# Layer 0's attention on one Trainium2 core: score and value products of 512 columns instead of 256

## The chip, the cores and the metric

The kernel runs as one program on one core of a Trainium2 chip. The metric is the device time of one execution in microseconds, lower is better; the time before is the median of three runs. In the text PE is TensorE (matrix products; PEld are its weight loads), DVE is VectorE, ACT is ScalarE, POOL is GpSimd and SP is the engine that issues most DMAs. PSUM is the memory that PE writes its results to.

## The reference, cut to what matters

Two transformer layers over 8 sequences of 256 tokens with 128 channels, all in fp32. Each layer adds an attention and a mixture of experts, both of the same normalised input. The change touches only the attention of layer 0, with 16 heads of 8 channels:

```python
q, k, v = (proj(Wq, bq), proj(Wk, bk), proj(Wv, bv))     # (B, H=16, S=256, D=8)
scores = jnp.einsum('bhsd,bhtd->bhst', q, k) / jnp.sqrt(jnp.float32(D))
attn = jax.nn.softmax(scores, axis=-1)
out = jnp.einsum('bhst,bhtd->bhsd', attn, v)
x = x + out.reshape(B, S, E) @ Wo + bo + layer0_experts(xn)
```

Layer 0's experts (two of eight per token, and a shared one) and the whole of layer 1 (attention with 8 heads of 128 channels, one of eight experts per token) stay as they are.

## The kernel before

**Heads as rows.** The projections give queries and keys turned, channels on the 128 partitions and tokens along the row. The weight columns are reordered so that partition 32j + 8g + d holds channel d of head 4g + j: four bands of 32 partitions (j), each with four groups (g) of 8 channels. A score product of one head runs on one band of PE, 32 rows high, so four products on different bands can run at the same time. As a band holds four heads, `l0_project` writes four masked copies of the queries and four of the keys, one per group, with the other groups' rows put to zero by a column of ones and zeros (`own`). A block of 512 tokens (two sequences) therefore has 2 x 4 copies of 128x512. For block 0 DVE makes the queries' and ACT the keys' copies, for block 1 ACT makes all eight, for blocks 2 and 3 ACT copies the PSUM result once for each of the two (L566) and POOL makes the eight copies (L569).

**Two passes.** For the softmax's maximum, `max_scores` (L894) computes the scores with queries on the partitions and `max_rows` (L909) reduces them to minus the maximum, which goes into `mx`. `l0_augment` turns `mx` by two PE transposes (L918), and four DVE instructions (L921), one per group, add the maximum of a group to the queries in rows that belong to the next group; the copies of the keys hold ones in these rows (`turn`), so the second score product (`exp_scores`, L940) comes out with the maximum already taken off. ACT takes exponentials of 128x1024 at a time (L952). `l0_pv` (L967) multiplies them by the values. A value product has only 32 columns of weights, so four products run side by side on the columns of PE; they take 32 columns from `va_flat`, which are a head's 8 values, a one for the softmax's sum, and the next heads' columns, which are not used. `l0_normalise` turns the result by a DVE transpose in blocks of 32 and divides by the sum.

**The order.** For each sequence b there are eight units i (group g and half, a half being two bands). A unit issues four maximum products of sequence b + 1 and four score products of sequence b on the other two bands, in two rounds of two and two (`issue`), each product 256 columns wide; then the maximum reduction on DVE and the exponential on ACT. The maximum products write one PSUM tile of 128x1024 and the score products another. The pool has two such tiles, both taken by a unit and taken over by the next, so that a unit's maximum products wait for the reduction of the unit before, and its score products for the exponential before. After the second unit of a group `late` is set, and the value products of that group run in the unit that follows (`l0_drain`).

**What lies between.** `plan` is a table, written by hand, of places (two to each unit) at which other work is put into the same in-order engine queues: routing at the first places, then the 39 tiles of layer 0's experts (`l0_tile`, about five tiles to four units: a down product L709, four up products L692, one transpose L685, with the ACT instructions L718, L676 and L687), then the shared expert (L745, L760), the gathers of expert results, the norm of layer 1 and its first projections (L807). At i = 2 and i = 4 of an even sequence the loop projects the next block's queries and keys (L561). Those small products share three PSUM banks in turn (`bank`), so that a new one waits for the reader of the third before it. `keep_warm` (L1009) puts in products whose result nobody reads.

**The beginning.** Before the loop the eight maximum units of sequence 0 are issued in pairs (`first_scores`), without score products. The last sequence has score products without maximum products. All instructions of an engine run in the order of the program.

Of the kernel before, what the change touches and what calls it, by code (L numbers as in the profile page):

```python
# [10 lines left out]
F32 = mybir.dt.float32  # L11
# [4 lines left out]
ALU = mybir.AluOpType  # L16
# [46 lines left out]
def two_layer_kernel(  # L63
# [85 lines left out]

    hb = ctile([P, 2], "hb")  # L150
# [6 lines left out]
    qkb = ctile([P, 2, NG], "qkb")  # L157
# [5 lines left out]
    for g in range(NG):  # L163
        at = D0 * ((g + 1) % NG)
        seq(nc.vector.tensor_reduce(
            turn[:, g : g + 1],
            ident.rearrange("p (j r) -> p j r", r=ROW)[:, :, at],
            AX.X,
            ALU.add,
        ))  # L170
# [368 lines left out]
    def l0_values(blk):  # L539
        for t2 in range(blk * TPB, (blk + 1) * TPB, 2):  # L540
            ps = bank(f"vg_{t2}")
            pv = ps[:, : 2 * (E + NE + 1)].rearrange("p (t c) -> p t c", t=2)
            for t in range(2):
                seq(nc.tensor.matmul(
                    pv[:, t, :], lhsT=xT[:, ts(t2 + t, P)], rhs=wvg0_s, start=True, stop=True
                ))
            for t in range(2):
                seq(nc.scalar.copy(
                    va[:, t2 + t, :, :D0], pv[:, t, :E].rearrange("p (h d) -> p h d", d=D0)
                ))  # L550
            seq(nc.vector.tensor_copy(lg0[:, ds(t2, 2), :], pv[:, :, E:]))

    def l0_project(blk, n):


        if n == 0:
            both = work.tile([P, 2, NG, BLK], F32, tag="qk", name=f"qk0_{blk}")
            qk[blk] = (both[:, 0], both[:, 1])
        dst = qk[blk][n]
        ps = bank(f"qk0_{blk}_{n}")  # L560
        seq(nc.tensor.matmul(  # L561
            ps, lhsT=(wq0_p, wk0_p)[n], rhs=xT[:, ts(blk, BLK)], start=True, stop=True
        ))
        if blk > 1:
            both = work.tile([P, BLK], F32, tag="xn", name=f"qk0_all_{blk}_{n}")
            seq(nc.scalar.copy(both, ps))  # L566
        for g in range(NG):
            if blk > 1 or (blk == 0 and n == 0):
                seq((nc.gpsimd if blk else nc.vector).tensor_scalar(  # L569
                    dst[:, g, :],  # L570
                    both if blk else ps,
                    own[:, g : g + 1],
                    qkb[:, n, g : g + 1],
                    ALU.mult,
                    ALU.add,
                ))
            else:
                seq(nc.scalar.activation(
                    dst[:, g, :],
                    ps,  # L580
                    AF.Identity,
                    bias=qkb[:, n, g : g + 1],
                    scale=own[:, g : g + 1],
                ))
# [299 lines left out]

    def max_scores(b, i, ps):

        g, half = divmod(i, 2)
        qT, kT = qk[b // 2]
        o = (b % 2) * S
        pv = ps.rearrange("p (j t k) -> p j t k", j=2, t=2)  # L890

        def mm(t, jj):
            r = ROW * (2 * half + jj)
            seq(nc.tensor.matmul(  # L894
                pv[:, jj, t, :],
                lhsT=qT[r : r + ROW, g, ds(o + t * P, P)],
                rhs=kT[r : r + ROW, g, ds(o, S)],
                start=True,
                stop=True,
            ))  # L900

        return [(mm, t, jj) for t in range(2) for jj in range(2)]

    def max_rows(b, i, ps):

        g, half = divmod(i, 2)
        pv = ps.rearrange("p (j t k) -> p j t k", j=2, t=2)
        m = mx[b % 2].rearrange("p t (j r) -> p j t r", r=ROW)
        seq(nc.vector.tensor_reduce(  # L909
            m[:, ds(2 * half, 2), :, D0 * ((g + 1) % NG)], pv, AX.X, ALU.max, negate=True  # L910
        ))

    def l0_augment(b):

        qT, _ = qk[b // 2]
        ps = bank(f"mT_{b}")
        for t in range(2):
            seq(nc.tensor.transpose(ps[:, ts(t, P)], mx[b % 2][:, t, :], ident))  # L918
        qa = work.tile([P, NG, S], F32, tag="h", name=f"qa_{b}")
        for g in range(NG):  # L920
            seq(nc.vector.scalar_tensor_tensor(  # L921
                qa[:, g, :],
                ps[:, :S],
                turn[:, g : g + 1],
                qT[:, g, ds((b % 2) * S, S)],
                ALU.mult,
                ALU.add,
            ))
        return qa

    def exp_scores(b, i, qa, ps):

        g, half = divmod(i, 2)
        _, kT = qk[b // 2]
        o = (b % 2) * S
        pv = ps.rearrange("p (j c q) -> p j c q", j=2, c=2)

        def mm(c, jj):
            r = ROW * (2 * half + jj)
            seq(nc.tensor.matmul(  # L940
                pv[:, jj, c, :],
                lhsT=kT[r : r + ROW, g, ds(o + c * P, P)],
                rhs=qa[r : r + ROW, g, :],
                start=True,
                stop=True,
            ))

        return [(mm, c, jj) for c in range(2) for jj in range(2)]

    def exponentials(b, i, ps):  # L950
        eT = work.tile([P, 2, 2, S], F32, tag="e", name=f"eT_{b}_{i}", bufs=4)
        seq(nc.scalar.activation(eT.rearrange("p j c q -> p (j c q)"), ps, AF.Exp, scale=SC0))  # L952
        return eT

    def issue(*lists):

        for n in range(0, 4, 2):
            for calls in lists:
                for f, *args in calls[n : n + 2]:
                    f(*args)  # L960

    def l0_pv(b, g, eTs, po):

        for c in range(2):
            for j in range(4):
                o = ((2 * b + c) * H0 + 4 * g + j) * VW
                seq(nc.tensor.matmul(  # L967
                    po[ds(ROW * j, ROW), ts(g % 2, S)],
                    lhsT=va_flat[:, ds(o, ROW)],
                    rhs=eTs[j // 2][:, j % 2, c, :],  # L970
                    start=(c == 0),
                    stop=(c == 1),
                ))
# [3 lines left out]
    def l0_normalise(b, gp, po, at):  # L977

        nm = f"{b}_{gp}"
        ot = work.tile([P, 2, NQ, ROW], F32, tag="c", name=f"ot0_{nm}")  # L980
        seq(nc.vector.transpose(ot.rearrange("p g n r -> p (g n r)"), po))
        rec = small.tile([P, 2, NQ], F32, tag="rec0", name=f"rec0_{nm}")
        seq(nc.vector.reciprocal(rec, ot[:, :, :, D0]))
        seq(nc.vector.tensor_tensor(
            at[:, :, ds(2 * gp, 2), :].rearrange("p n g d -> p g n d"),
            ot[:, :, :, :D0],
# [29 lines left out]
    def first_maxima(i, pair):  # L1016
# [11 lines left out]
    seq(nc.vector.tensor_scalar(qkb[:, 0, :], own, hb[:, 0:1], None, ALU.mult))  # L1028
    seq(nc.vector.scalar_tensor_tensor(
        qkb[:, 1, :], own, hb[:, 1:2], turn, ALU.mult, ALU.add  # L1030
    ))
# [4 lines left out]
    l0_project(0, 0)  # L1036
    l0_project(0, 1)
# [20 lines left out]
    pair = first_scores(6)  # L1058
    next(routing0)
# [16 lines left out]
    def l0_drain(b, g, eTs, po, at):  # L1076
        l0_pv(b, g, eTs, po)
        if g % 2 == 1:
            l0_normalise(b, g // 2, po, at)
# [4 lines left out]
    late = None  # L1084
    keep_warm(3)
    qa = l0_augment(0)
    for b in range(B):
        at = work.tile([P, NQ, NG, D0], F32, tag="at0", name=f"at0_{b}")
        for g in range(NG):
            if g % 2 == 0:  # L1090
                po = held(f"pv0_{b}_{g}")
            eTs = []
            for half in range(2):

                i, i1 = 2 * g + half, 2 * g + 1 - half
                place = 2 * (b * NI + i)
                lists = []
                if b + 1 < B:
                    ps1 = big_tile(f"s1_{b + 1}_{i1}")
                    lists.append(max_scores(b + 1, i1, ps1))  # L1100
                ps2 = big_tile(f"s2_{b}_{i}")
                issue(*lists, exp_scores(b, i, qa, ps2))
                if b + 1 < B:
                    max_rows(b + 1, i1, ps1)
                eTs.append(exponentials(b, i, ps2))
                between(place)
                if b % 2 == 0 and b + 2 < B and i in (2, 4):
                    l0_project(b // 2 + 1, i // 2 - 1)
                if i == NI - 1 and b + 1 < B:
                    qa = l0_augment(b + 1)  # L1110
                if half == 0 and late is not None:
                    l0_drain(*late)
                    if g == 1 and done is not None:
                        l0_finish(*done)
                        done = None
                if i == 1 and done is not None:
                    done = (done[0], l0_turn_back(*done))
                between(place + 1)
            late = (b, g, eTs, po, at)
        done = (b, at)  # L1120
# [473 lines left out]
```

## Time and profile before

| What | Value |
|---|---|
| runs, us | 594.53, 591.26, 590.09; median 591.26 |
| profiled execution, us | 584.82 |
| its span, us | 583.0 |
| mean granted PE clock | 0.938 |
| PE, PEld busy, us | 497.3, 354.1 |
| DVE, ACT, POOL busy, us | 359.4, 246.6, 205.6 |
| PE instructions in the profile | 3996 products and 3996 weight loads |

The span is the time from the first to the last instruction of the profiled execution; 1.8 us of its time lie outside. Every fp32 product of the program appears as two records, each with a weight load and the full number of columns. A row of the groups gives line, engine, operation, tiles and shapes, the count, the busy time in us, the mean duration of one in ns, and then the idle time of the engine just before these instructions with what ended it. Products overlap, so that the count times the mean is more than the busy time where several run side by side.

### The profile page before, as it was taken

What the parts mean: (1) busy time and instruction counts of PE and PEld (TensorE: products, weight loads), DVE (VectorE), ACT (ScalarE), POOL (GpSimd) and SP (SyncE); (2) the same over time, 40 slices, a digit from 0 to 9 for tenths busy, and PEclk for the clock granted to TensorE, in tenths of its full rate; (3) what the DMA queues carried; (4) which work ended last, traced back from release to release, by engine and by line L of the source; (5) the groups of instructions that cost most, each with busy time, mean ns of one, the idle gap of its engine ahead of it and who ended that gap; (6) DMA issues with size and microseconds to landing.
All of it is one profiled execution on the core that took longest, in us unless ns stands there. A gap on an engine that the chain in (4) does not pass through costs nothing.

```text
span 583.0 us, 11267 instructions
## 1 busy us (share of the span) xinstructions
PE 497.3 (85%) x3996; PEld 354.1 (61%) x3996; DVE 359.4 (62%) x733; ACT 246.6 (42%) x681; POOL 205.6 (35%) x254
## 2 busy tenths in 40 slices
PE   4887688889998899967899968877969989989777
PEld 1633345656766577543554736666667878978666
DVE  5487954646756467637797467787633544527662
ACT  4616123434443254313443551523255584665161
POOL 6230023266432440274372032212576041124740
PEclk9999786989999799989999997996989999999977
DMA  3600411324443231011021130171048465512111
GB/s 108 189 1 19 133 33 44 110 72 121 126 128 105 74 77 38 28 46 29 17 69 45 37 92 19 37 200 41 25 108 234 145 149 180 158 55 64 33 32 56
DMA packets 61925, 47.78 MB, mean 82 GB/s; under 512 B 6389, under 2 KB 56781, under 8 KB 61869
## 3 DMA queue, kind: packets, MB, share of 16 engines
q1 hardware_dynamic: 57453, 38.59, 23.3%
q0 software_dynamic: 3840, 8.26, 5.9%
q8 instruction: 32, 0.52, 0.4%
q10 hardware_dynamic: 576, 0.20, 0.1%
q14 instruction: 24, 0.20, 0.1%
HBM read 38.78 MB, written 8.26 MB: 81 GB/s over the span
## 4 chain that ended last, share of the span: by engine, by line
PE 56%; DVE 20%; issue 9%; ACT 6%; POOL 4%; DMA 1%; SPq 0%; another core or an unknown queue 0%; POOLq 0%; ACTq 0%; DVEq 0%
PE s L894 7%; PE u L692 6%; PE pv L967 5%; PE s L1281 4%; PE d L709 4%; DVE mx L909 4%; PE u L1210 3%; PE o L1345 3%; PE d L1228 3%; PE qk L807 3%; PE s L940 3%; PE wo L1364 3%; ACT p L1301 2%; PE ds L760 2%; PE sh L745 2%
## 5 line engine op out<-in xcount | busy, mean ns | idle before, releaser
L952 ACT ACTIVATE eT<-s 128x1024 f32<-128x1024 f32 x64 | 65.5, 1024 | 138.9 <-PE s L940 95.7
L909 DVE TENSOR_REDUCE mx<-s 128x4 f32<-128x1024 f32 x64 | 77.7, 1220 | 32.0 <-PE s L940 14.3
L513 POOL DMA_INDIRECT xs<-xd,idx x62 | 63.0, 1016 | 67.0 <-issue 57.8
L894 PE MATMUL s<-qk 32*128 32x256 f32 x512 | 74.4, 422 | 13.6 <-DVE mx L909 8.8
L1313 POOL TENSOR_TENSOR p<-p,rec 128x1024 f32<-128x1024 f32 x21 | 39.8, 1896 | 112.3 <-DVE rec L1311 112.2
L1301 ACT ACTIVATE p<-s,m 128x256 f32<-128x256 f32 (+1 forms) x128 | 52.5, 443 | 62.5 <-DVE m L1295 51.0
L940 PE MATMUL s<-qa,qk 32*128 32x256 f32 x512 | 75.6, 414 | 2.5 <-DVE qa L921 2.3
L894 PEld LDWEIGHTS s<-qk 32*128 32x128 f32 x512 | 43.2, 195 | 41.7 <-DVE mx L909 17.9
L513 POOL DMA_INDIRECT yt<-yg,idx x48 | 48.9, 1020 | 47.1 <-issue 37.2
L1281 PE MATMUL s<-kT,qT 128*128 128x128 f32 (+1 forms) x256 | 49.8, 348 | 9.1 <-ACT p L1301 4.3
L940 PEld LDWEIGHTS s<-qa,qk 32*128 32x128 f32 x512 | 45.9, 192 | 10.6 <-DVE qa L921 5.0
L1345 PE MATMUL o<-pT,vrep 32*128 32x256 f32 x576 | 48.9, 407 | 3.9 <-DVE pT L1328 2.2
L1281 PEld LDWEIGHTS s<-kT,qT 128*128 128x128 f32 x256 | 40.0, 200 | 18.2 <-issue 6.9
L1345 PEld LDWEIGHTS o<-pT,vrep 32*128 32x128 f32 x576 | 40.5, 197 | 11.6 <-DVE pT L1328 2.4
L692 PE MATMUL u<-xg,gu_s 128*88 128x128 f32 x312 | 42.6, 278 | 1.6 <-issue 1.6
L967 PE MATMUL pv<-eT,va 128*32 128x256 f32 x512 | 39.3, 412 | 1.5 <-issue 1.4
L692 PEld LDWEIGHTS u<-xg,gu_s 128*88 128x88 f32 x312 | 37.1, 160 | 3.8 <-issue 3.8
L1219 ACT ACTIVATE h<-u,own_b 128x128 f32<-128x128 f32 x92 | 25.9, 375 | 27.7 <-PE u L1210 25.2
L1291 DVE TENSOR_TENSOR s<-s,mask 128x512 f32<-128x512 f32 (+1 forms) x24 | 20.9, 869 | 25.2 <-PE s L1281 21.5
L1364 PE MATMUL wo<-wo_s,oT 128*128 128x128 f32 x256 | 34.0, 297 | 2.1 <-DVE qT L814 1.8
L1364 PEld LDWEIGHTS wo<-wo_s,oT 128*128 128x128 f32 x256 | 33.0, 212 | 3.9 <-issue 3.3
L1328 DVE STREAM_TRANSPOSE pT<-p 128x1024 f32<-128x1024 f32 x24 | 29.5, 1232 | 7.1 <-POOL p L1313 7.1
(222 smaller groups left out, 843.2 us busy)
## 6 DMA issues: line engine op xcount, KB each, us to landing
w_up<-in_w_dram SPq DMA_DIRECT2D x30, 256.0 KB
gu_s<-in_gu_dram SPq DMA_DIRECT2D x39, 176.0 KB
vrep<-vd SPq DMA_DIRECT2D x32, 128.0 KB
w_down<-in_w_dram SPq DMA_DIRECT2D x16, 256.0 KB
yg<-ys SPq DMA_DIRECT2D x14, 256.0 KB
dn_s<-in_dn_dram SPq DMA_DIRECT2D x39, 88.0 KB
bias<-in_b_dram SPq DMA_DIRECT2D x23, 64.0 KB
acc<-in_x_dram SPq DMA_DIRECT2D x4, 256.0 KB
```

The source lines that it names most:

```text
L513: seq(nc.gpsimd.indirect_dma_start(out=dst, out_offset=None, in_=table, in_offset=bass.IndirectOffsetOnAxis(ap=idx[:, k : k + 1], axis=0), ...
L692: seq(nc.tensor.matmul(ps[:IC, ts(c, P)], lhsT=gu0_s[:, i % RING0, c, :], rhs=xg0.get(i), start=True, stop=True,))
L894: seq(nc.tensor.matmul(pv[:, jj, t, :], lhsT=qT[r : r + ROW, g, ds(o + t * P, P)], rhs=kT[r : r + ROW, g, ds(o, S)], start=True, stop=True,))
L909: seq(nc.vector.tensor_reduce(m[:, ds(2 * half, 2), :, D0 * ((g + 1) % NG)], pv, AX.X, ALU.max, negate=True))
L940: seq(nc.tensor.matmul(pv[:, jj, c, :], lhsT=kT[r : r + ROW, g, ds(o + c * P, P)], rhs=qa[r : r + ROW, g, :], start=True, stop=True,))
L952: seq(nc.scalar.activation(eT.rearrange("p j c q -> p (j c q)"), ps, AF.Exp, scale=SC0))
L967: seq(nc.tensor.matmul(po[ds(ROW * j, ROW), ts(g % 2, S)], lhsT=va_flat[:, ds(o, ROW)], rhs=eTs[j // 2][:, j % 2, c, :], start=(c == 0), s ...
L1281: seq(nc.tensor.matmul(u.sc[:, h, :], lhsT=qT[:, u.h0 + h, ds(o + u.t * P, P)], rhs=kT[:, ds(o, u.nk)], start=True, stop=True,))
L1301: seq(nc.scalar.activation(u.p[:, h, :], u.sc[:, h, :], AF.Exp, bias=u.m[:, h : h + 1], accum_out=u.sums[:, h : h + 1],))
L1313: seq(engine.tensor_tensor(u.p, u.p, rec[:, : u.nh].unsqueeze(2).to_broadcast([P, u.nh, u.nk]), ALU.mult))
L1345: seq(nc.tensor.matmul(po[n][:, ts(t, H1 * ROW)], lhsT=vrep[r : r + ROW, b % 2, j, :], rhs=pT[r : r + ROW, :, j, :], start=(j == 0), stop= ...
L1364: seq(nc.tensor.matmul(ps[:, ts(t, P)], lhsT=oT[:, h, ts(t, P)], rhs=wo1_s[:, h, :], start=(h == 0), stop=(h == H1 - 1),))
```

## The change

The unit of work becomes two groups of heads side by side. The query side is left unmasked for the maximum (one tile of 128x512 for a block, `l0_queries`), and the keys are masked in two ways (`l0_keys`): four copies by group (`kg`), of which two stand side by side as the moving operand of a maximum product, and two copies by pair of groups (`k2`), which are the weights of the score product. The queries of the score product are masked by group for each sequence by four ACT instructions of 128x256 (`l0_own_queries`), one in each of the units 1 to 4 of the sequence before, and the maximum is added in place by the same four DVE instructions as before. Maxima now go to the rows of the other pair of groups. A unit (`unit`: pair n, half of the tokens t or c, half of the bands) has two maximum and two score products of 512 columns each. Value products take 512 columns as well, two groups of one band side by side, with the values reordered so that both heads' columns lie next to each other; the two results of a band then lie in different rows, and `l0_normalise` reads the second with an offset of 9. The masked keys are made by ACT for all blocks, after block 0 one copy to a unit, and POOL takes no more part in it. The key projection moves from unit 4 to unit 3.

```diff
-    def l0_project(blk, n):
-        if n == 0:
-            both = work.tile([P, 2, NG, BLK], F32, tag="qk", name=f"qk0_{blk}")
-            qk[blk] = (both[:, 0], both[:, 1])
...
-        if blk > 1:
-            both = work.tile([P, BLK], F32, tag="xn", name=f"qk0_all_{blk}_{n}")
             seq(nc.scalar.copy(both, ps))
-        for g in range(NG):
-            if blk > 1 or (blk == 0 and n == 0):
-                seq((nc.gpsimd if blk else nc.vector).tensor_scalar(
...
+    def l0_queries(blk):
+        both = work.tile([P, 1 + NG + NG // 2, BLK], F32, tag="qk", name=f"qk0_{blk}")
+        qk[blk] = (both[:, 0], both[:, 1 : 1 + NG], both[:, 1 + NG :])
+        ps = bank(f"q0_{blk}")
+        seq(nc.tensor.matmul(ps, lhsT=wq0_p, rhs=xT[:, ts(blk, BLK)], start=True, stop=True))
+        seq(nc.scalar.activation(qk[blk][0], ps, AF.Identity, bias=hb[:, 0:1]))
+
+    def l0_keys(blk):
+        ps = bank(f"k0_{blk}")
+        seq(nc.tensor.matmul(ps, lhsT=wk0_p, rhs=xT[:, ts(blk, BLK)], start=True, stop=True))
+        if blk:
+            both = work.tile([P, BLK], F32, tag="xn", name=f"k0_all_{blk}")
+            seq(nc.scalar.copy(both, ps))
+            ps = both
+            yield
+        _, kg, k2 = qk[blk]
+        copies = [(kg[:, g, :], own[:, g : g + 1], kb[:, g : g + 1]) for g in range(NG)]
+        copies += [(k2[:, n, :], own2[:, n : n + 1], kb2[:, n : n + 1]) for n in range(NG // 2)]
+        for n, (dst, scale, bias) in enumerate(copies):
+            if blk == 0 and n < 2:
+                seq(nc.vector.tensor_scalar(dst, ps, scale, bias, ALU.mult, ALU.add))
             else:
+                seq(nc.scalar.activation(dst, ps, AF.Identity, bias=bias, scale=scale))
+            if blk:
+                yield
+
+    def l0_own_queries(b, g):
+        seq(nc.scalar.activation(
+            qas[b % 2][:, g, :],
+            qk[b // 2][0][:, ds((b % 2) * S, S)],
+            AF.Copy,
+            scale=own[:, g : g + 1],
+        ))
...
+    def unit(i):
+        return i // 4, i // 2 % 2, i % 2
...
-        def mm(t, jj):
+        def mm(jj):
             r = ROW * (2 * half + jj)
             seq(nc.tensor.matmul(
-                pv[:, jj, t, :],
-                lhsT=qT[r : r + ROW, g, ds(o + t * P, P)],
-                rhs=kT[r : r + ROW, g, ds(o, S)],
+                ps[:, ts(jj, 2 * S)],
+                lhsT=qT[r : r + ROW, ds(o + t * P, P)],
+                rhs=kg[r : r + ROW, ds(2 * n, 2), ds(o, S)],
...
-                lhsT=kT[r : r + ROW, g, ds(o + c * P, P)],
-                rhs=qa[r : r + ROW, g, :],
+                lhsT=k2[r : r + ROW, n, ds(o + c * P, P)],
+                rhs=qa[r : r + ROW, ds(2 * n, 2), :],
...
-    def l0_pv(b, g, eTs, po):
-        for c in range(2):
-            for j in range(4):
-                o = ((2 * b + c) * H0 + 4 * g + j) * VW
-                seq(nc.tensor.matmul(
-                    po[ds(ROW * j, ROW), ts(g % 2, S)],
-                    lhsT=va_flat[:, ds(o, ROW)],
-                    rhs=eTs[j // 2][:, j % 2, c, :],
+    def l0_pv(b, n, c, eTs, po):
+        for j in range(4):
+            o = ((2 * b + c) * H0 + NG * j + 2 * n) * VW
+            seq(nc.tensor.matmul(
+                po[ds(ROW * j, ROW), :],
+                lhsT=va_flat[:, ds(o, ROW)],
+                rhs=eTs[j // 2][:, j % 2].rearrange("p g q -> p (g q)"),
...
+            if b + 1 < B and NG > i - 1 >= 0:
+                l0_own_queries(b + 1, i - 1)
+            if b % 2 == 0 and b + 2 < B and i == 2:
+                l0_queries(b // 2 + 1)
+            if b % 2 == 0 and b + 2 < B and i == 3:
+                keys = l0_keys(b // 2 + 1)
+            if keys is not None:
+                next(keys, None)
             if i == NI - 1 and b + 1 < B:
                 qa = l0_augment(b + 1)
             if half == 0 and late is not None:
                 l0_drain(*late)
```

The four own queries of sequence 0 are made before the loop, after the last pair of maximum units is issued. The value products still run once in two units, and number half as many.

## The prediction

> **What bounds the kernel now.** I read the profile from the whole to the stage: first busy time by stretches, then the costliest groups, then the order of time inside one unit, then what PE waited for. Layer 0's attention runs from about 36 to 333 us. This view has one line for each stretch: length, then busy us and instructions of PE, PEld, DVE, ACT and POOL, PE clock, DMA share, GB/s.
>
> ```profile
> 36.00:88.00 52.00, 39.53 (x340) 19.58 (x339) 40.76 (x102) 16.76 (x19) 8.59 (x10) 0.89 0.18 52
> 88.00:216.00 128.00, 115.98 (x1098) 82.46 (x1099) 75.49 (x140) 52.95 (x129) 54.99 (x66) 0.92 0.36 96
> 216.00:333.00 117.00, 105.41 (x836) 62.27 (x836) 81.34 (x174) 45.27 (x83) 44.24 (x58) 0.99 0.15 39
> ```
>
> From 88 to 333 us PE is busy 221.4 of 245 us, so PE sets the pace there. From 36 to 88 us (routing) DVE and PE take turns. ACT works less than half of each stretch. What the change must shorten is therefore PE's own time, or the 23.6 us that PE still waits after 88 us.
>
> ```profile
> L894 PE MATMUL s<-qk 32*128 32x256 f32 x512 | 74.4, 422 | 13.6 <-DVE mx L909 8.8
> L940 PE MATMUL s<-qa,qk 32*128 32x256 f32 x512 | 75.6, 414 | 2.5 <-DVE qa L921 2.3
> L967 PE MATMUL pv<-eT,va 128*32 128x256 f32 x512 | 39.3, 412 | 1.5 <-issue 1.4
> L894 PEld LDWEIGHTS s<-qk 32*128 32x128 f32 x512 | 43.2, 195 | 41.7 <-DVE mx L909 17.9
> ```
>
> These are the products concerned. L894 and L940 lie over each other (512 x 422 ns would be 216 us), so their sum isn't PE's cost. The timeline of one unit (start, us, what) says how they run:
>
> ```profile
> 139.57 0.48 PE L894 MATMUL s<-qk 32*128 32x256 f32 x2
> 139.58 0.48 PE L940 MATMUL s<-qa,qk 32*128 32x256 f32 x2
> 139.89 0.38 PE L894 MATMUL s<-qk 32*128 32x256 f32 x2
> 139.90 0.38 PE L940 MATMUL s<-qa,qk 32*128 32x256 f32 x2
> 140.10 0.38 PE L894 MATMUL s<-qk 32*128 32x256 f32 x2
> ...
> 140.32 0.38 PE L894 MATMUL s<-qk 32*128 32x256 f32 x2
> ...
> 140.65 0.71 PE L709 MATMUL d<-dn_s,h 88*128 88x128 f32 x4
> ```
>
> Sixteen records go in four rounds of four, all four bands at once. A round takes 0.215 us (139.89 to 140.10 to 140.32), the first 0.32, and the next work starts 0.33 after the last: 1.08 us in all, of which 4 x 0.215 = 0.86 are columns and 0.22 belong to start and end. Weight loads of the next round lie under the running one.
>
> **The products (the heart of the change).** A unit will have 8 records of 512 columns, two rounds of four. What does a record of 512 columns take? The chain of waits has six in a row:
>
> ```profile
> 488.80 2.58 PE qk L807 x6
> ```
>
> 2.58 / 6 = 0.43 us, twice 0.215. So the unit is 2 x 0.43 + 0.22 = 1.08 us, as before. Value products: 16 records in four rounds now, 8 in two rounds then, 0.86 us either way, in 32 calls. The weight loads halve (768 of 3996 go), but all but the first of each unit are covered by a running round, and the first stays. If each round has a few ns of its own, two rounds less in 64 units and 32 calls are 192 x 3 ns, about 0.5 us; I take -0.5.
>
> Here a rule of the Trainium skill says otherwise: "TensorE: Matmul & The Clock Gate", section "Back-to-back issue gap", gives a sustained spacing of 81 ns per product at 128 columns and 131 ns at 512, so wide products would be far cheaper per column. Estimate by that page: about 98 ns at 256 columns, two of these against 131, a third less; of 0.86 us x (64 + 32) = 83 us that would be -27 us. The row above (0.43 against 0.215) decides: cost per column is the same here.
>
> **The wait for the queries of the next sequence.** At each turn of sequence PE waits for L921, four DVE instructions 0.39 us apart:
>
> ```profile
> 147.21 0.70 PE L894 MATMUL s<-qk 32*128 32x256 f32 x4
> 147.94 1.65 DVE L921 SCALAR_TENSOR_TENSOR qa<-mT,turn,qk 128x256 f32<-128x256 f32 x4
> 148.47 0.19 PEld L940 LDWEIGHTS s<-qa,qk 32*128 32x128 f32 x2 [0.95 <-DVE qa L921]
> ```
>
> The first score product reads one group and starts 0.53 us after the first of the four. Now its moving operand is two groups, so it starts after the second: +0.39 us. What PE has left then is the same: before, 1.06 us (148.47 to 149.53); after, both maximum products have run alone and the score products take two rounds, 1.08. Behind this wait on PE's queue stand the expert tile, the value products and the next unit. In six of the eight turns (from 36, 73, 110, 147, 183 and 221 us) the products began 0.53 us after the first L921, so were held by it; in the last two PE was late for other reasons. 6 x 0.39 = +2.4 us.
>
> **ACT.**
>
> ```profile
> L578 ACT ACTIVATE qk<-qk,qkb,own 128x512 f32<-128x512 f32 x12 | 8.4, 776 | 2.3 <-PE qk L561 2.3
> L566 ACT COPY qk_all<-qk 128x512 f32<-128x512 f32 x4 | 2.3, 586 | 3.5 <-PE qk L561 3.5
> L569 POOL TENSOR_SCALAR qk<-qk_all,own,qkb 128x512 f32<-128x512 f32 x16 | 12.2, 777 | 18.0 <-ACT qk_all L566 18.0
> ```
>
> Own queries: 32 of 128x256. No such row is there; L676 (256 wide, no scale by column) takes 0.381 us and L1301's 256 wide form 0.509. I take 0.49, nearer to the latter, as both read a column: +15.7 us. Blocks 2 and 3: one query copy (0.68, between L566 and L578), one L566 (0.586) and six copies of 0.776 are 5.9 us in place of 2 x 0.586 = 1.2, so +9.4 for two. Block 1: 5.9 in place of 8 x 0.776 = 6.2, -0.3. Block 0: five in place of four, +0.7, but the query copy falls into ACT's gap at 13.0 to 13.8 us, while DVE loses two of its four. ACT gets +25.5 us, POOL loses 12.2 us.
>
> How much comes out? ACT lies on PE's way where PE waits for a PSUM bank or for an exponential. From 88 to 216 us:
>
> ```profile
> PE s L894 <- issue: 4.6, 2, 3.9
> PE qk L561 <- ACT ys L718: 4.1, 2, 2.4
> ...
> PE mT L918 <- ACT ys L718: 1.3, 2, 0.6
> PE d L709 <- ACT ys L718: 0.7, 1, 0.7
> ```
>
> PE waited 6.1 us for 52.95 us of ACT's work, 11.5%. The same share of 25.5 is +2.9 us. The own queries stand after the expert tile's ACT work and ahead of the next exponential; where ACT is idle there, nothing comes out (end 0), and where none is hidden, all 25.5. I stay near the lower end since ACT is busy only 41% of that stretch. Section "Rules for kernel authors" of the skill's "ScalarE: Activation LUTs" speaks against this placing: multiply and add belong on VectorE, up to about three times faster there (said of bf16). The trace's four fp32 copies of the same shape on DVE took 0.796 us each (L569's DVE form) against 0.776 on ACT. By the rule up to two thirds of this time were wasted (17 us of work, about 2 of the path); by the row nothing.
>
> **The rest.** DVE's reductions keep 128x1024 in and 4 numbers out (1.220 us). POOL's work on keys was off PE's way; without it the gathers behind it may start earlier, worth 0 to -1 us; I take 0. The key projection moves one unit ahead on PE and past DVE's routing work; same work, 0. Four small sums and biases on DVE at the start fall into its wait for the input (1.55 us at 3.7 us), 0.
>
> **Sum.** -0.5 + 2.4 + 2.9 = +4.8 us: 584.8 becomes 589.6 for the profiled execution. The runs shown have their median 6.4 us above it; I carry the difference over: 591.3 + 4.8 = 596.1, say 596 us.
>
> **Rivals.** (1) *ACT becomes the bound* in the units that hold an own query, a key copy and two expert tiles: own query 0.49 + copy 0.78 on top of about 2.2 us of exponential and tile work make 3.5 of a unit of 4.4. For: the bank waits above. Against: half the units have neither. If half of 25.5 comes out, 12.7 + 1.9 = +14.6: 606 us. It decides once more than a quarter of it comes out. (2) *The wide products don't run four abreast.* If two rounds become three, 0.43 x 96 = +41: 632 us. Against: nothing in a unit shares a band or bank. (3) *Faster*, the other side: the waits of PE go. Half as many instructions end the 4.6 us of "issue" before L894 and the 1.4 before L967, and shorter-held banks the 4.1 us before L561: -10 + 2.4 with ACT hidden, 583.7 us. For: those waits stand in the profile. Against: the largest (3.9) is a single event and no row ties it to the number of products.
>
> **Chances.** Forecast 0.57 (its own range 592 to 600), rival 1 0.24 (600 to 612), rival 2 0.05, rival 3 0.14. About 1% is what the measurement can tell from no change, 585.3 to 597.2: of the forecast 0.45 lie inside, 0.10 above, 0.02 below; of rival 3 0.03 inside. Faster 0.13, same 0.48, slower 0.39. Range 584 to 606: it leaves out rival 2 (0.05), half of rival 1 and the lower part of rival 3, about 0.2.
>
> **What would show it.** A full unit still 1.05 to 1.10 us with starts 0.43 apart, PE's busy time from 88 to 333 us unchanged within 3 us, PEld down by a sixth; L921 waits longer by 0.39 per turn; ACT at about 272 us busy. Starts less than 0.4 apart would refute the heart of this; longer waits for ACT in front of L561, L709 and the exponentials would mean rival 1.

## The result, and the profile after

The changed kernel took 589.6 us (median of 20 runs) against 587.9 us for the kernel before (20 runs), +1.6 us. Three runs of each kernel were slow, and over the fast ones alone, as for every ratio below, the ratio is 1.0062, 95% interval 1.0036 to 1.0087, or +3.7 us (2.1 to 5.1). The two comparisons lie 2 us apart, so the size of the change is known no better than that. The profiled execution took 588.2 us, 584.8 before.

Runs fell on several chips: on chips of a first kind (numbers 0 and 14 below) the kernel before takes 584 to 588 us, on chips of a second kind (4, 9 and 10) 547 to 548 us. Both kernels above were measured at the times of the first kind. Each ratio below is to the kernel before on the same chip. Each of the five numbered chips has one set of runs only, so a property of the chip is not told apart from one of the hour.

The groups of the changed kernel's page that answer to the products shown before:

```profile
L912 PE MATMUL s<-qk 32*128 32x512 f32 x256 | 72.8, 679 | 12.7 <-DVE mx L926 11.2
L956 PE MATMUL s<-qa,qk 32*128 32x512 f32 x256 | 76.1, 671 | 4.0 <-DVE qa L943 4.0
L982 PE MATMUL pv<-eT,va 128*32 128x512 f32 x256 | 37.6, 662 | 0.0
L912 PEld LDWEIGHTS s<-qk 32*128 32x128 f32 x256 | 19.3, 193 | 43.7 <-DVE mx L926 21.7 <-issue 7.4 <-DVE sg L692 4.0
```

Half as many products (256 in place of 512) are busy for the same time: 72.8, 76.1 and 37.6 us against 74.4, 75.6 and 39.3. The loads of L912 fall from 43.2 to 19.3 us, and the products' own time does not fall with them. The wait for `qa` in front of the score products grows from 2.3 to 4.0 us. A full unit in the timeline (start, us):

```profile
173.96 0.70 PE L912 MATMUL s<-qk 32*128 32x512 f32 x2
173.97 0.70 PE L956 MATMUL s<-qa,qk 32*128 32x512 f32 x2
...
174.49 0.59 PE L912 MATMUL s<-qk 32*128 32x512 f32 x2
174.50 0.59 PE L956 MATMUL s<-qa,qk 32*128 32x512 f32 x2
```

Two rounds of four, from 173.96 to 175.09: 1.13 us. The four rounds of the unit shown before ran from 139.57 to 140.70, 1.13 us too. The same stretches as before (length, then busy us and instructions of PE, PEld, DVE, ACT and POOL, PE clock, DMA share, GB/s):

```profile
36.00:88.00 52.00, 43.72 (x204) 13.27 (x206) 40.57 (x104) 19.00 (x25) 6.66 (x7) 0.84 0.17 47
88.00:216.00 128.00, 113.91 (x782) 65.94 (x774) 74.71 (x139) 63.63 (x149) 46.75 (x55) 0.96 0.38 99
216.00:333.00 117.00, 105.90 (x558) 49.40 (x553) 81.81 (x176) 49.20 (x93) 43.04 (x56) 0.96 0.13 36
```

From 88 to 333 us PE is busy for 219.8 us, 221.4 before. ACT has 10.7 us more from 88 to 216 us. PE's waits for it there, and for its own instructions:

```profile
PE q L568 <- ACT ys L733: 3.5, 2, 1.8
PE mT L940 <- ACT ys L733: 2.1, 2, 1.5
...
PE s L912 <- issue: 1.5, 2, 0.8
PE u L707 <- ACT sg L691: 1.3, 1, 1.3
...
PE d L724 <- ACT ys L733: 0.3, 1, 0.3
```

The waits for ACT are 7.2 us in place of 6.1: those behind `ys` 5.9, and one new wait of 1.3 in front of an expert's up product. The wait put down to issue in front of the maximum products is 1.5 in place of 4.6 us.

### The profile page after: what moved, and what is told of

Same layout as the page of the kernel before. It is cut to its first block, busy times and chain, and to the rows that moved or that the text cites. A ratio compares the mean times of both kernels' runs of the same rounds, so it can differ in the third digit from the quotient of the medians.

```text
span 586.0 us, 9748 instructions
## 1 busy us (share of the span) xinstructions
PE 502.0 (86%) x3228; PEld 316.7 (54%) x3228; DVE 357.1 (61%) x733; ACT 267.9 (46%) x726; POOL 194.0 (33%) x238
## 4 chain that ended last, share of the span: by engine, by line
PE 55%; DVE 22%; issue 8%; ACT 6%; POOL 3%; DMA 1%; another core or an unknown queue 0%; SPq 0%; POOLq 0%; ACTq 0%; DVEq 0%
PE s L912 8%; PE u L707 5%; PE pv L982 5%; DVE mx L926 4%; PE o L1373 4%; PE d L724 4%; PE s L1309 3%; PE qk L822 3%; PE u L1238 3%; PE s L956 3%; PE d L1256 3%; ACT p L1329 3%; PE wo L1392 3%; PE ds L775 2%; PE sh L760 2%
## 5 line engine op out<-in xcount | busy, mean ns | idle before, releaser
L912 PE MATMUL s<-qk 32*128 32x512 f32 x256 | 72.8, 679 | 12.7 <-DVE mx L926 11.2
L956 PE MATMUL s<-qa,qk 32*128 32x512 f32 x256 | 76.1, 671 | 4.0 <-DVE qa L943 4.0
L912 PEld LDWEIGHTS s<-qk 32*128 32x128 f32 x256 | 19.3, 193 | 43.7 <-DVE mx L926 21.7
L692 DVE SCALAR_TENSOR_TENSOR sg<-sg,u 88x256 f32<-88x256 f32 x39 | 16.3, 417 | 37.5 <-ACT sg L691 29.6
L982 PE MATMUL pv<-eT,va 128*32 128x512 f32 x256 | 37.6, 662 | 0.0
L724 PEld LDWEIGHTS d<-dn_s,h 88*128 88x128 f32 x156 | 21.0, 195 | 29.8 <-issue 15.2
```

The lines of the kernel that those rows point to most:

```text
L724: seq(nc.tensor.matmul(ps[:, :P], lhsT=h0[i][:, c, :], rhs=dn0_s[:, i % RING0, c, :], start=(c == 0), stop=(c == 1),))
L912: seq(nc.tensor.matmul(ps[:, ts(jj, 2 * S)], lhsT=qT[r : r + ROW, ds(o + t * P, P)], rhs=kg[r : r + ROW, ds(2 * n, 2), ds(o, S)], start=Tr ...
L956: seq(nc.tensor.matmul(ps[:, ts(jj, 2 * S)], lhsT=k2[r : r + ROW, n, ds(o + c * P, P)], rhs=qa[r : r + ROW, ds(2 * n, 2), :], start=True, ...
L982: seq(nc.tensor.matmul(po[ds(ROW * j, ROW), :], lhsT=va_flat[:, ds(o, ROW)], rhs=eTs[j // 2][:, j % 2].rearrange("p g q -> p (g q)"), star ...
```

## Theories

*Theory.* Products and ACT cost nothing; three delays make the loss: block 0's key copies at the start, the longer wait at each turn of sequence, and a PSUM bank at the turn to sequence 7. *Rival:* the recorded sum, turn +2.4 and ACT +2.9. *Rival:* the products themselves, in either direction. On the first kind of chip the timelines of the two kernels differ by -4 to +4 us from unit to unit, so most is read on the second kind, where most of the units that are alike take the same time to 0.02 us.

## The experiments

**Both kernels again, on the second kind.**

> The kernel before, unchanged, for a profile on the chip of these runs: the ratio to itself is 1.000 within its interval. Its times of the exponentials, unit by unit, are what the other runs of this call are set against.

> The changed kernel, unchanged, for a profile on the same chip. Ratio to the kernel before 1.004 to 1.009, as measured. Theory: unit by unit against the kernel before, +1.9 us at the first exponential, +0.47 us at each turn of sequence (4.84 against 4.37 us, or 4.46 against 3.99), +2 to +3.5 us at the turn to sequence 7, and equal steps of 2.70 and 5.37 us elsewhere; somewhere between there must be a gain of about 5 us, else the sum would be +8 to +9.

Measured on chip 4: the kernel before against itself 1.0025 (1.0000 to 1.0051), which is how far two sets of runs can lie apart; the changed kernel 1.0090 (1.0057 to 1.0122). Starts of ACT's exponentials in the profiles, us; the last two columns are kernels that come later (repaired: `mended_third`; repaired with 256 columns: `mended_narrow_2`):

| sequence, unit | before | changed | repaired | repaired, 256 |
|---|---|---|---|---|
| 0, 0 | 37.31 | 39.90 | 38.17 | 37.83 |
| 2, 0 | 103.81 | 105.15 | 101.21 | 105.96 |
| 6, 0 | 233.99 | 236.35 | 231.00 | 235.85 |
| 6, 6 | 259.60 | 261.88 | 256.49 | 261.40 |
| 7, 0 | 271.87 | 277.65 | 268.92 | 273.81 |
| 7, 7 | 302.43 | 307.53 | 298.79 | 303.73 |

From (2, 0) to (6, 0), 32 units: 130.18 before, 131.20 changed. The turns to sequences 2, 3, 4 and 5 take 4.84 us each in the changed kernel and 4.37 before (the turn to 2 lies ahead of this stretch). The other steps are equal or cancel in pairs: 3.56 and 5.32 in place of 2.70 and 6.19 in the even sequences. These 0.86 us are the two records of the key projection (0.43 us each), which moved by one unit (`keys_pool` below bears this out). From 88 to 216 us PE waits for ACT nowhere, in either kernel. From (6, 6) to (7, 0): 12.27 before, 15.77 changed, +3.5 us. So the products and ACT show no cost here, and no gain of 5 us between the exponentials either.

From (2, 0) to (7, 7) it is 198.62 us before, 202.38 changed, 197.58 repaired and 197.77 repaired with 256 columns. What lies outside depends on the clock. The routing, from (0, 0) to (2, 0), took 63 to 68 us in the eleven profiles of the second kind, and the work behind the last exponential, nearly all of it layer 1, which no edit touches, 239 to 244 us; it was 3.0 us shorter in the changed kernel's profile than in that of the kernel before. In slices of 0.2 us the granted clock of all twenty profiles falls to 0.50 in stretches of 3.41 us or a multiple, 35 to 85 us of each execution: 58 us in this profile of the kernel before, 48 in that of the changed one, 35 in the repaired. So the rows of the table up to (2, 0) show luck with the clock as well as the kernels.

**Two banks for block 0's keys.**

```diff
+        if blk == 0:
+            ps_dve = bank("k0_dve")
+            seq(nc.tensor.matmul(ps_dve, lhsT=wk0_p, rhs=xT[:, ts(blk, BLK)], start=True, stop=True))
...
-                seq(nc.vector.tensor_scalar(dst, ps, scale, bias, ALU.mult, ALU.add))
+                seq(nc.vector.tensor_scalar(dst, ps_dve, scale, bias, ALU.mult, ALU.add))
```

> Block 0's keys come from two projections in two PSUM banks, one read by DVE's two copies and one by ACT's four. Theory: in the changed kernel the first ACT copy of the keys waits for the two DVE copies (1.9 us), and this delay is carried to the end; with two banks ACT's copies start about 1.9 us earlier, the first maximum products start near 17.8 us instead of 19.7, and the time falls by 1.5 to 2 us against the changed kernel (ratio to the kernel before about 1.003). Rival: the start is only moved into the routing stage, where DVE has the pace, and the time stays (1.006). The recorded sum put this step at nothing.

Measured: 1.0041 (1.0014 to 1.0067), chip 9, second kind. The timelines of the start (start, us, and in brackets the idle time and what ended it), kernel before, changed, two banks:

```profile
12.09 2.94 DVE L569 TENSOR_SCALAR qk<-qk,own,qkb 128x512 f32<-128x512 f32 x4
...
13.31 2.79 ACT L578 ACTIVATE qk<-qk,qkb,own 128x512 f32<-128x512 f32 x4 [0.52 <-PE qk L561]
```

```profile
13.89 1.53 DVE L586 TENSOR_SCALAR qk<-k,own,kb 128x512 f32<-128x512 f32 x2 [3.53 <-PE k L575]
...
15.45 2.79 ACT L588 ACTIVATE qk<-k,kb,own 128x512 f32<-128x512 f32 x4 [2.58 <-DVE qk L586]
...
18.29 0.62 PEld L553 LDWEIGHTS vg<-wvg_s,xT 128*128 128x128 f32 x4 [3.00 <-ACT qk L588]
```

```profile
13.90 2.78 ACT L591 ACTIVATE qk<-k,kb,own 128x512 f32<-128x512 f32 x4 [0.93 <-PE k L575]
```

Before, DVE and ACT copied from two banks at the same time. In the changed kernel ACT's four copies begin when DVE's two are done, and PE's next weight load waits 3.00 us for ACT. That the common bank is the cause shows in this run, where nothing else changes and DVE and ACT copy at the same time again. ACT starts 1.55 us earlier, the first exponential moves from 39.90 to 38.34 us and the last from 307.53 to 305.94, so the profile carries the gain through the routing. The times agree in direction (0.49% less than the 1.0090 of chip 4, 2.7 us), but the two intervals overlap.

**The first unit split by group.** At i = 0 alone, score products of 256 columns, group by group:

```diff
+        if i == 0:
+            return [(one_group, g, jj) for g in range(2) for jj in range(2)]
         return [(mm, jj) for jj in range(2)]
```

> The score products of the first unit of each sequence are split by group again, 256 columns each, so that the first waits for one of the four DVE instructions only. Recorded sum: 6 turns of 0.39 us, -2.4 us against the changed kernel (ratio to the kernel before about 1.002). Theory that the turn was hidden by other delays: 0 (1.006). In both the wait of the first score product at a turn should shrink from about 0.95+0.39 to 0.95 us.

Measured: 1.0003 (0.9978 to 1.0028), chip 9, against 1.0090 on chip 4. Turn to sequence 4, changed kernel and split:

```profile
168.85 1.65 DVE L943 SCALAR_TENSOR_TENSOR qa<-mT,turn,qa 128x256 f32<-128x256 f32 x4
...
169.87 1.13 PE L956 MATMUL s<-qa,qk 32*128 32x512 f32 x4 [0.87 <-DVE qa L943]
```

```profile
169.40 1.13 PE L966 MATMUL s<-qa,qk 32*128 32x256 f32 x8 [0.38 <-DVE qa L943]
```

The first score product starts 1.02 us after the first DVE instruction, with the split 0.53; the turns to sequences 2 to 5 fall from 4.84 to 4.37 us. These four give 1.9 us; the 4.8 us between the ratios are more. The clock may hold a part: set against the kernel before on the same chip, the mean granted clock was 0.0016 higher with the split and 0.0015 lower without it, which is an estimated 3.4 us at half clock and 1.7 us of time.

**Layer 1's first values one place later**, so that the down products get another bank:

```diff
-        at_place(n + 6, l1_values, blk)
+        at_place(n + 6 + (blk == 0), l1_values, blk)
```

> The values of layer 1's first block are computed one place later, so that the shared expert's third down product gets the PSUM bank that was read long before, and no longer that of layer 1's key projection. Theory: at the turn to sequence 7 the changed kernel's 24 down products wait 1.9 us for DVE's reading of that projection and then run partly at half clock; without it the time falls by 2 to 3.5 us (ratio to the kernel before 1.000 to 1.003). Rival: PE would have waited at this turn anyway for the DVE work behind it, 0 to -0.5 us (1.005 to 1.006).

Measured: 1.0105 (1.0063 to 1.0148), six runs on chip 9; the expected gain did not come. The turn to sequence 7 did shrink, from 10.88 to 8.77 us, but the profile has two other steps of 6.99 in place of 5.37 us (unit 1 of sequences 3 and 4). Such a step was profiled in `double_own` too; its window and that of the same unit in the changed kernel (clock behind the POOL column):

```profile
140.30:147.30 7.00, 7.00 (x44) 4.61 (x45) 3.51 (x9) 3.30 (x9) 0.00 (x0) 0.76 0.28 72
```

```profile
138.50:144.00 5.50, 5.50 (x44) 3.57 (x45) 3.52 (x9) 3.32 (x9) 0.00 (x0) 1.00 0.35 92
```

Same 44 products, PE busy throughout, clock 0.76 against 1.00: a stretch at half clock of 3.4 us costs 1.6 us where PE is the bound. What starts one isn't shown. On the second kind this step of 6.99 us stands behind a turn in two of the four profiles whose first unit has wide score products, and in none of the seven in which they are 256 columns wide there, so the longer wait may favour it, but does not always bring it.

**Score and maximum products split** (with the values later): `[(mm, g, jj) for g in range(2) for jj in range(2)]` in both functions, 256 columns each, and `issue` back in rounds of two and two.

> As values_later, but every maximum and score product is split into two of 256 columns, as many products as in the kernel before, in the order of the kernel before; value products stay at 512. Recorded view (0.215 against 0.43 us): the same as values_later within 1 us, less the turn wait of about 2 us, since the first score products need one group only, so -1 to -2 us. Rival, the rule by which wide products are cheaper per column: two thirds of 27 us more, +18 us. Rival, that every product has a small fixed cost: +1 to +4 us.

Measured: 1.0022 (0.9998 to 1.0046), chip 9. This is 4.5 us below the wide `values_later` where 1 to 2 were expected, and the profile has no step of 6.99 us; the turns to sequences 2 to 5 are 4.37 us, as in `first_split`. By the rule that the expectation names, the spacing cited in the prediction, it would have been 18 us slower (an estimate).

**Own queries made twice.** `for _ in range(2):` around the ACT instruction.

> Each own query copy on ACT is made twice (the second writes the same values again): 32 more ACT instructions of about 0.4 us, 13 us of ACT work. Recorded sum (11.5 per cent of ACT's added work comes out): +1.5 us against the changed kernel. Theory that they are hidden: 0 to +0.5 us. Rival 1 of the record (ACT becomes the bound, half comes out): +6 us or more.

Measured: 1.0112 (1.0057 to 1.0166), six runs on chip 4, against 1.0090 (1.0057 to 1.0122) there. The ratios can't tell 1.5 us from nothing, but the steps can. Those without a turn and without half clock are the changed kernel's (2.70, 5.20, 5.32): 16 us more of ACT's work (32 x 0.507) add no step that the profile shows, and no wait of PE for ACT from 88 to 216 us.

**Three repairs at once** (two banks, first unit split, values later).

> The changed kernel with all three: two banks for block 0's keys, the first unit's score products split by group, layer 1's values one place later. Theory (the three losses add up): -1.9, -3.3 and -2.1 us, so -5 to -7 us against the changed kernel and a ratio to the kernel before of 0.995 to 0.998. Rival (they are absorbed by DVE's routing or by half-clock stretches): ratio 1.000 or more, as values_later alone gave 1.0105.

Measured: 0.9989 (0.9961 to 1.0016), chip 4. Together the repairs give 1.0% less than the changed kernel on the same chip, 5.5 us, within the 5 to 7 expected. The turn to 7 still takes 8.77 us where 7.39 were taken before; there the second transpose of the maxima waits 0.88 us for DVE, which the values had covered.

**Values one place earlier** (`n + 6 - (blk == 0)`), alone.

> Only the values of layer 1's first block are moved, one place ahead, so that the shared expert's third down product gets a bank whose readers are long done, and nothing new stands between the transposes of the maxima and these down products. Theory: the step of the exponentials at the turn to sequence 7 falls from 10.88 to about 7.0 to 7.5 us (7.39 in the kernel before), the time by about 3 us against the changed kernel, ratio to the kernel before about 1.003. Rival (the wait moves to DVE's work behind it): step 8.8 or more, gain 2 us or less.

Measured: 0.9930 (0.9898 to 0.9962), chip 0, first kind. Down products (L760, L775, L778) of the kernel before, the changed kernel and the repaired kernel of the table:

```profile
266.90 2.94 PE L760 MATMUL ds<-shd_s,hs 128*128 128x128 f32 x24
```

```profile
271.05 4.57 PE L775 MATMUL ds<-shd_s,hs 128*128 128x128 f32 x24 [1.89 <-DVE kT L829]
```

```profile
264.04 2.85 PE L778 MATMUL ds<-shd_s,hs 128*128 128x128 f32 x24
```

In the changed kernel the 24 products had been given the bank of layer 1's key projection, waited 1.89 us for DVE to read it, and then ran partly at half clock (4.57 us; the granted clock is 0.57 from 271 to 275 us). The wait and the 1.63 us by which they run longer make the 3.5 us of this turn. With values earlier they start at once. From (6, 6) to (7, 0): 12.41 us in this kernel, 15.77 in the changed one. The time fell by more (1.3%, 7.8 us, against a ratio that was measured elsewhere) than this step's 3.4 us; where the rest comes from isn't shown.

**All three, with this placing.**

> The three repairs together, with this placing of the values: two banks for block 0's keys, the first unit's score products split by group, values one place ahead. Theory (three losses and no gain from the products): the exponentials within 1.5 us of the kernel before at every unit after the routing, and the ratio 0.995 to 1.000. If the wide products had a gain of their own it would now be seen: ratio below 0.993.

Measured: 0.9946 (0.9912 to 0.9979), chip 0: faster than the kernel before, but no faster than the values alone, 0.9930 on the same chip. So in these runs the second bank and the split add nothing that can be seen. The exponentials were not within 1.5 us of the kernel before ((3, 0) at 153.26 us against 149.65, in profiles of different sets of runs).

**Keys back on POOL** (`nc.gpsimd.tensor_scalar` for blocks 2 and 3).

> The key copies of blocks 2 and 3 go back to POOL, as in the kernel before: ACT loses 12 instructions of 0.78 us, 9.4 us of work, POOL gets them. Recorded sum (11.5 per cent comes out): -1.1 us against the changed kernel. Theory that ACT's added work is hidden: 0, with the step to unit 4 of sequences 2 and 4 back from 3.56 to 2.70 us and the next one from 5.32 to 6.19. Rival (POOL's work on keys held back the gathers): +1 us or more.

Measured: 1.0029 (1.0000 to 1.0059), chip 0, against 1.0062 (1.0036 to 1.0087). The intervals overlap, so it tells neither 0 from -1.1 us nor more. The step to unit 4 of sequences 2 and 4 did not move back: it is 3.56 us with POOL making the keys too. So it belongs to the projection that moved one unit ahead, and not to ACT's copies.

**Why the repaired kernel leads.** Four on one chip of the first kind: the repaired kernel; the same with both kinds of score product split; the same without the split at turns; and the kernel before with values earlier.

> The three repairs once more, as the reference of this call: 0.993 to 0.999 of the kernel before.

> As mended, but all maximum and score products are two of 256 columns, as many as in the kernel before. View that the width is worth nothing by itself: the same as mended within 0.3 per cent. View that PE waits for its own instruction stream on a chip of the first kind (588 us; waits put down to issue of 4.6, 1.6 and 1.4 us before, 1.5, 0.7 and 0 after), and that half as many products end it: on such a chip 3 to 5 us slower than mended, on a chip of the second kind (548 us) the same. The rule that wide products are much cheaper per column: +18 us on any chip.

> As mended, but without the split of the first unit: the score products of a turn wait for two DVE instructions again. The steps at the turns give 4 to 5 x 0.47 = 1.9 to 2.4 us more than mended; if the longer wait at a turn also brings half-clock stretches behind it (the step of 6.99 in place of 5.37 us seen in values_later and double_own), 3 to 6 us more.

> The kernel before with layer 1's first values one place ahead, the one repair that it could share. If this placing is worth something without the change: 1 to 3 us faster than the kernel before, ratio 0.995 to 0.998, and then mended owes its lead to it. If not: 1.000 within the interval.

Measured on chip 14: 0.9902 (0.9866 to 0.9938), 1.0096 (1.0062 to 1.0129), 0.9944 (0.9912 to 0.9977), 1.0019 (0.9978 to 1.0061). The moved values bring nothing without the change. The turn costs 0.42%, 2.5 us (overlapping intervals). The split costs 1.96%, 11 us, with intervals far apart, and more than twice the 3 to 5 us expected. The clock holds a part of it: its mean was 0.943 in the repaired kernel's runs and 0.937 in the split one's, an estimated 8 us more at half clock, worth at most 4 of the 11. ACT's waits for exponentials that no instruction of the trace explains ("remote": us in total, times, longest), from 36 to 340 us, of the kernel before, the repaired and the split one:

```profile
ACT eT L952 <- remote: 9.4, 2, 6.3
```

```profile
ACT eT L983 <- remote: 9.5, 1, 9.5
```

```profile
ACT eT L971 <- remote: 19.9, 3, 12.7
```

All waits put down to "remote" or "issue" on PE, DVE and ACT in this stretch are 41 us before, 24 in the changed kernel, 32 in the repaired and 45 in the split one. Over all nine profiles of the first kind, the three kernels whose score and maximum products have 256 columns have 41 to 45 us of them and the six with 512 have 23 to 33. These are sums over three engines, not time lost, and they do not rank the kernels: `mended_turn` has the fewest and is not the fastest. In the eleven profiles of the second kind there is none.

**The same on the second kind**, with a version that splits the score products alone.

> The repaired kernel again, as reference. On a chip of the first kind (kernel before at 584 to 588 us) 0.990 to 0.995 of the kernel before; on one of the second kind (548 us), where units without a turn take the same time in both kernels, 0.995 to 0.999.

> As mended, with the score products alone in two of 256 columns and the maximum products at 512, so that half of the 512 records come back. If the number of products sets the loss on a chip of the first kind: half of the 9 to 11 us, 4 to 6 us slower than mended. If it is a threshold, or owed to the maximum products: 0 or all of it. On a chip of the second kind: within 0.3 per cent of mended.

> As mended, with all maximum and score products in two of 256 columns, a second time. On a chip of the first kind 9 to 11 us slower than mended, as before. On a chip of the second kind within 0.3 per cent of mended: then the loss belongs to the kind of chip, and not to the products themselves.

Measured on chip 10: 0.9933 (0.9908 to 0.9958), 0.9956 (0.9931 to 0.9982), 0.9943 (0.9916 to 0.9969): all alike, and ahead of the kernel before by somewhat more than expected. In the table the 32 units take 129.79 us repaired and 129.89 split. So the products' own time does not depend on their width, and the 11 us came only at the times of the first kind. Whether that loss grows with the number of products was not tried there. The lead here goes with the clock: its mean was 0.963 in the repaired kernel's runs and 0.954 in those of the kernel before, an estimated 10 us less at half clock, worth up to 5 us where the lead is 3.7. From (2, 0) to (7, 7) the repaired kernel is only 1.0 us shorter.

## Why the prediction was right or wrong

**What failed.** A slower kernel was forecast and came, but of the three terms of the sum only the turn was right. ACT's +2.9 us came out as nothing on the second kind and as 1.1 us of waits on the first; "the rest", put at 0, held two losses of 1.6 to 2.6 and 3.5 us; and rival 3, which had a part in it, was set aside. That +4.8 us lies near the measured difference is luck. In the profiles of the second kind the changed kernel's last exponential is 5.1 us late for other reasons: +2.6 us at the first exponential, -1.25 over the routing, where the clock plays in, and +3.8 from there, nearly all of it at the turns.

**The base.** 596 us was 6.4 above the 589.6 measured. 3.3 of these are in the 6.4 us between the profiled execution and the median of three runs, which were carried over: over 20 runs this kernel's median lies only 3.1 us above its profiled execution. The other 3.1 are the difference of the medians, 1.6 us instead of 4.8. The difference by the ratio, 3.7 us (2.1 to 5.1), would have allowed 4.8.

**The products (-0.5).** The heart held: a unit of 1.13 us before and after, PE's busy time within 3 us, and no effect of width on the second kind. There the spacing of the Trainium skill ("TensorE: Matmul & The Clock Gate", section "Back-to-back issue gap"), of which the prediction estimated 27 us for all products, would have made the kernel with split score and maximum products about 18 us slower (two thirds, an estimate); measured was none. The -0.5 itself rested on 3 ns a round, for which no row was given. PEld fell by 11%, not by a sixth. At the times of the first kind the split did cost 11 us. That fits what rival 3 named (half as many instructions end the waits for issue), and here the step that failed is its dismissal, "the largest (3.9) is a single event and no row ties it to the number of products". How a product costs time there is open: its rounds are no longer, but waits without a releaser are more, and up to 4 of the 11 us may be the clock's. The split changes the order of issue and the number of weight loads too, and half a split was measured on the second kind alone. The split kernel is also 0.96% slower than the kernel before there (5.6 us), with fewer products than that has; this too is open.

**The turn (+2.4).** Right in its mechanism: 0.47 us a turn where 0.39 were forecast, plain at four turns on the second kind (1.9 us), buried at the turn to sequence 1 by the routing and absent at that to 6; 2.5 us by `mended_turn`, with overlapping intervals. One of the six turns was misread: at 73 us the products began 0.62 us after the first L921 and show no wait for it. A stretch of half clock behind the turn, seen in two profiles, was not in the sum.

**ACT (+2.9).** The work was sized well: the rows of the change grew from 10.7 to 37.6 us, +26.9 where 25.5 was forecast. ACT's busy time, in which records that overlap count once, grew by 21.3 us to 267.9. The step that failed is the share of 11.5%. On the second kind PE waits for ACT from 88 to 216 us neither before nor after, the steps are equal, and doubled own queries add none. On the first kind PE waited 7.2 us in place of 6.1, which the share would give as well (11.5% of 10.7 is 1.2), but the waits do not follow ACT's work: they are highest, 12.3 us, in `keys_pool`, where ACT has 9.4 us less to do, and 9 to 11 us in the repaired kernels. So a cost of ACT on the first kind is not excluded, and what sets it is open.

**"The rest" (0).** The step that failed most. "The query copy falls into ACT's gap" was true of that copy (12.18 to 12.87 us), but counted instructions per engine and not which bank each reads: of the key copies behind it DVE's and ACT's now read one. The first exponential comes 2.6 us later; a second bank gives back 1.6, and the other 1.0 is open. This stood in the diff, where `l0_keys` hands one `ps` to both engines. And "same work, 0" passed over which tile follows which in a bank: the down products at the turn to 7 got the bank of a projection not yet read, +3.5 us (1.9 of wait and 1.6 of half clock behind it).

**The rivals.** ACT as the bound and products not four abreast are refuted by the steps. Rival 3, a faster kernel, is partly right: with the two losses repaired, and the turn, the changed kernel is 0.5 to 1.0% faster than the one before on both kinds. On the first kind the moved values alone give as much, on the second the lead goes with the clock; how much of it belongs to the products is not shown.

## What to carry to other kernels

When an edit moves which engine reads what, list for each PSUM bank its readers and the next writer, before and after: two readers of one bank, or a bank handed on while its reader is still queued, cost 1.6 and 3.5 us here, and 21 us of added busy time on an engine with gaps cost nothing that could be seen. A share of an engine's busy time is no measure of what its waits will cost. When a large change moves the time little, repair its side losses one by one before judging its idea. And set a forecast of time on many runs, with the clock beside them: the three-run median cost half of the 6.4 us.

## What was not expected of the hardware

The same program took 547 to 548 us on some chips and 584 to 588 on others. The difference lies largely in layer 0's attention (the last exponential at 302.43 against 334.00 us before). Waits without a releaser stand only in the profiles of the slower chips, and only there did the split products cost time. The clock falls to half in stretches of 3.41 us or a multiple, at places that differ between runs, in all twenty profiles, also while PE is busy throughout; one such stretch moves the time by up to 1.6 us, as much as each of the effects sought.
